# Row statistics moved by one row, and one scaling moved by one product, in a single-core graph attention kernel

## Chip, core and metric

One Trainium2 chip, of which one core is used. The metric is the device time of one execution in microseconds. A core has five engines that run beside each other, each through a list of instructions in a fixed order: TensorE (PE, with its weight loads PEld), VectorE (DVE), ScalarE (ACT), GpSimd (POOL) and SyncE (SP), which here issues nearly all DMA transfers. An instruction waits for semaphores of other engines; whatever stands behind it on its engine waits with it.

## What is computed

```
h = max(layernorm(x, over 768 features), 0)              # x: 128 graphs x 128 nodes x 768, float32
q, k, v = h @ Wq + bq, h @ Wk + bk, h @ Wv + bv          # 12 heads of 64, seen as 8 batches of 1024 rows
s = q k^T / sqrt(64) + beta * adj                        # within each graph: adj is 128 x 128 x 128
s = -9e15 where adj <= 0
out = x + softmax(s) v
```

In the kernel the unit is a graph of 128 nodes: attention runs between the nodes of one graph.

## The kernel before

**Groups, slices, products.** Four graphs make a group G; there are 32 groups, 0 to 31. For each group the three projections are computed in three slices: `qk0` (queries and keys of the first six heads), `v`, and `qk1` (queries and keys of the other six). The text calls them the first, second and third slice. From group 1 on a slice is 15 *products* (`product_z`, L521; the table at L66) of a fast matrix multiplication: each multiplies a prepared sum of blocks of the activations with a prepared sum of blocks of the weights, in 7 zones of two matmuls (28 instructions of TensorE, line L537). A product belongs to one of four *chains* a, b, c, d. A chain adds all its products up in one PSUM pair (two banks), and after each of its products the running sum is added to, or copied into, one or two of the six results (`home`) of the slice. So the next product of the same chain, usually three places later, can start only when that has been done: PSUM must have been read before TensorE adds to it again.

**Reading PSUM out.** The first product that goes into a result copies it with ScalarE (L555 for five zones and two times L557, with the bias, in the q and k slices; L551 on VectorE and L552 on ScalarE in the second slice). Later products are added by VectorE (L561). When all products of a result are there, GpSimd decodes it (L577 to L580 for q and k, L588 to L592 for v; one of them per group on VectorE).

**PSUM pairs.** There are four in all, in a queue: `take` gets the oldest free one, `give` puts one back. Chains hold one from their first to their last product; scores and weighted sums take one for a short time.

**Attention of a group.** Scores (L614) are 32 matmuls behind a product. VectorE caps them, adds the mask and frees the pair (L622); ScalarE takes the exponential (L624). The weighted sums (`attend_steps`, L671) are woven into the zones of the next product; then ScalarE copies the row sums and the values out of PSUM (L680, L682) and frees the pair; one product later VectorE takes the reciprocal (L642) and ScalarE scales the result with it in 8 instructions (L654); some products later VectorE adds `x` (L696) and SP sends the result to memory (L700). The last argument of `attention` (`behind`) is the number of products after which the addition comes; the sending comes two later. With 5 or less the scaling follows in the product of the reciprocal; with 6 it follows one product later (L688 and L689).

**Layer normalization of the groups to come.** From group 2 on it is spread over the slices of the two groups before. For each of the four graphs of group G+2 one row of `x` (128 x 768, 384 KB) is loaded into one buffer (`load_row`, L402, on SP), and ScalarE takes its statistics there (`row_stats`: L409 the sum, L410 the mean, L411 the squares). The next row can be loaded only when the statistics of the last one are through. When all four are there, `row_moments` makes them into scale and shift (L416 on VectorE, L421 and L422 on GpSimd) and turns them into the layout of the blocks by a write to memory and a broadcast read (L427 `turned`, L428 `block`, both on SP, a given number of products after the call). In the next group, ScalarE applies them to the blocks of `x` (`norm`, L438), which were loaded separately (`load_x`, L189). VectorE transposes the blocks (L449), GpSimd and VectorE make the sums that the products need (L459 to L461, L454).

**Weights.** Of the 45 prepared weight sums 11 stay on chip; the other 34 are streamed from memory for each group, 448 KB each, into a ring of five buffers (`load_T`, L335): a buffer is loaded again when its product is through.

**What sets the order.** From the second slice of group 0 on, the order on each engine is the order in which the program issues the instructions. A slice is a list `todo` of work by product number: `then(n, f)` issues f behind the matmuls of product n, ahead of the reading out of that product; `then((n, "post"), f)` issues it behind the reading out and behind what trails it (the scaling L654, the exponential L624). `later(f, k)` issues f k products on. `run` (L784) walks through a slice:

```
for at, steps in enumerate(products):
    next(steps)                    # matmuls, with woven-in weighted sums; then the load of weights
    behind_product(at, todo)       # todo[at], masks, L680/L682, then what is due from later()
    next(steps)                    # L555/L557 or L551/L552 or L561
    trail()                        # L654, L624
    for f in todo.get((at, "post"), ()):
        f()
```

The change touches only the numbers in the loop over the groups, L1039 to L1109.

Of the kernel before, what the change touches and what calls it, by code (L numbers as in the profile page):

```python
# [125 lines left out]
def direct(ctx, tc, x, adj, wq, bq, wk, bk, wv, bv, beta, out, bad):  # L126
# [14 lines left out]
    NG = B // GRP  # L141
# [181 lines left out]
    def order_of(G, sl):  # L323
        return LORDER if G == NG - 1 and sl == "qk1" else ORDER[sl]
# [459 lines left out]
    def run(products, todo):  # L784
        for at, steps in enumerate(products):
            next(steps)
            behind_product(at, todo)
            next(steps)
            trail()
            for f in todo.get((at, "post"), ()):  # L790
                f()

    def slice_z(G, sl, todo):
        run([product_z(G, sl, n) for n in order_of(G, sl)], todo)
# [163 lines left out]
    def then(at, f, *args):  # L958
        todo.setdefault(at, []).append(lambda: f(*args))
# [9 lines left out]
    def attention(G, u, at, behind=5):  # L969
        for n, j in at:  # L970
            then(n - 3, load_xo, G, 3 * u + j)
            then((n, "post"), attend, G, 3 * u + j, behind)
# [12 lines left out]
    def sums_at(G, slots):  # L985
        for at, name in slots:
            then(at, sum_acts, G, name)
# [51 lines left out]
    for G in range(1, NG):  # L1039
        more = G + 1 < NG  # L1040
        todo.clear()
        then(3, scores, G - 1, 1, 2)
        then(5, scores, G - 1, 1, 0)
        then((6, "post"), scores, G - 1, 1, 1)
        attention(G - 1, 1, ((7, 2), (10, 0), (12, 1)))
        if G == 1:
            sums_at(1, ((0, "S6"), (1, "S7"), (2, "S0"), (5, "S5"), (7, "S14"), (9, "S11")))
            then((0, "post"), load_x, 2, 0)
            for g, at in enumerate((3, 7, 11)):
                then((at, "post"), row_stats, 2, g)  # L1050
                then((at, "post"), load_row, 2, g + 1)
        else:
            sums_at(G, ((0, "S7"), (1, "S0"), (4, "S5"), (7, "S14"), (9, "S11")))
            if more:
                for g in range(2):
                    for h in range(2):
                        then((2 * g + h, "post"), norm, G + 1, g, 2 * h, 2 * h + 2)
                turn_act(G + 1, ((8, "A01"), (9, "A00"), (11, "A02")), None)
                then((12, "post"), load_x, G + 1, 1)
                if G + 2 < NG:  # L1060
                    then((12, "post"), load_row, G + 2, 0)
        slice_z(G, "qk0", todo)

        todo.clear()
        then(0, scores, G, 0, 2)
        then(2, scores, G, 0, 1)
        then(7, scores, G, 0, 0)
        if more:
            then((11, "post"), add_raw, G + 1)
            if G == 1:  # L1070
                then((0, "post"), row_stats, 2, 3)
                then(1, row_moments, 2, 3, 4)
                for n, at in enumerate((6, 7, 8, 9)):
                    then((at, "post"), norm, 2, n // 2, n % 2 * 2, n % 2 * 2 + 2)
                turn_act(2, ((10, "A01"), (11, "A00"), (12, "A02")), 1)
                then((12, "post"), load_x, 2, 1)
            else:
                for n, at in enumerate((3, 4, 7, 8)):
                    then((at, "post"), norm, G + 1, 2 + n // 2, n % 2 * 2, n % 2 * 2 + 2)
                turn_act(G + 1, ((10, "A11"),), 1)  # L1080
                for at, name in ((4, "A01"), (5, "A00"), (6, "A02")):
                    then(at, inner, G + 1, name)
            if G + 2 < NG:
                if G == 1:
                    then((1, "post"), load_row, 3, 0)
                for g, at in enumerate((5, 10, 14) if G == 1 else (1, 5, 10)):
                    then((at, "post"), row_stats, G + 2, g)
                    if at < 14:
                        then((at + 1, "post"), load_row, G + 2, g + 1)
        slice_z(G, "v", todo)  # L1090

        todo.clear()
        if not more:
            break
        attention(G, 0, ((3, 2), (9, 1), (12, 0)))
        if G == 1:
            for n, at in enumerate((0, 1, 2, 3)):
                then((at, "post"), norm, 2, 2 + n // 2, n % 2 * 2, n % 2 * 2 + 2)
            turn_act(2, ((4, "A10"), (5, "A11"), (6, "A12")), 1)
            then((0, "post"), load_row, 3, 3)  # L1100
        else:
            turn_act(G + 1, ((1, "A10"), (4, "A12")), 1)
        sums_at(G + 1, ((6 + (G == 1), "S1"), (7 + (G == 1), "S9"), (8 + (G == 1), "S2"), (11, "S6"), (13, "S10")))
        bias(G + 1, 0, 2, 4)
        if G + 2 < NG:
            then((4, "post"), row_stats, G + 2, 3)
            then(7, row_moments, G + 2, 3, 6)
            then((6, "post"), load_x, G + 2, 0)
        slice_z(G, "qk1", todo)  # L1109

    for at, f, *args in (
# [149 lines left out]
```

## Time and profile before

| | |
|---|---|
| runs | 2769.48 us median of 3 (2767.8 to 2770.46) |
| profiled execution | 2771.61 us, span of its trace 2769.8 us |
| busy: TensorE / weight loads | 2681.8 us (97%) / 2566.1 us (93%) |
| busy: VectorE / ScalarE / GpSimd | 2166.7 us (78%) / 1764.1 us (64%) / 2098.4 us (76%) |
| granted TensorE clock | 0.997 |
| DMA | 721.72 MB, 261 GB/s on average |

A group takes about 84 us: 84.60 us and 84.10 us for the two groups from 1556.60 us and from 1641.10 us, of which TensorE is busy for 82.39 and 82.41. In the timeline a row has the start, the duration, the engine, the line, the operation, output and input, the number of instructions in it, and in brackets the idle time of the engine before it with what ended it. Consecutive matmuls overlap (a row of one product lasts 1.70 us, yet the next starts 1.53 us after it), so lost time of TensorE is read from the distances between starts.

### The profile page before, as it was taken

The numbers are of one execution on the slowest core, as the hardware profiler recorded it, in microseconds if no ns is written. First come the engines' busy times: TensorE is split into PE (matmuls) and PEld (weight loads), VectorE is DVE, ScalarE is ACT, GpSimd is POOL, SyncE is SP. The second block draws the span as 40 slices with busy tenths as digits, with TensorE's granted clock in tenths as the row PEclk, the third lists the DMA queues.
The fourth block names the chain that finished last, engine by engine and source line by source line (L and its number), as shares of the span: only waits on it lengthen the run. The fifth ranks groups of instructions, "written<-read, shape, count | busy, mean of one in ns | idle before, by whom it ended". The sixth has DMA issues, their size and how long they took to land.

```text
span 2769.8 us, 121511 instructions
## 1 busy us (share of the span) xinstructions
PE 2681.8 (97%) x52029; PEld 2566.1 (93%) x52029; DVE 2166.7 (78%) x2693; ACT 1764.1 (64%) x4612; POOL 2098.4 (76%) x3046
## 2 busy tenths in 40 slices
PE   9989999999999999999999999999999999999997
PEld 7789999999999999999999999999999999999997
DVE  6868877777877778877788777778777888777885
ACT  1476666666666766666666666666667666666653
POOL 4767778777778777787777787777777777877774
PEclk9999999999999999999999999999999999999999
DMA  8788889888888888888888888888888888888875
GB/s 214 259 257 260 263 262 275 264 264 271 256 274 273 263 265 266 265 274 264 270 264 263 267 272 266 267 261 254 273 264 270 267 265 260 273 265 275 248 230 161
DMA packets 530341, 721.72 MB, mean 261 GB/s; under 512 B 105980, under 2 KB 374024, under 8 KB 529800
## 3 DMA queue, kind: packets, MB, share of 16 engines
q1 hardware_dynamic: 528640, 713.12, 83.9%
q8 instruction: 412, 6.75, 0.9%
q10 hardware_dynamic: 1160, 0.79, 0.2%
q14 instruction: 129, 1.06, 0.1%
HBM read 647.73 MB, written 66.05 MB: 258 GB/s over the span
## 4 chain that ended last, share of the span: by engine, by line
PE 59%; DVE 12%; ACT 12%; POOL 7%; issue 4%; DMA 3%; SPq 0%; ACTq 0%; DVEq 0%; POOLq 0%
PE pair L537 49%; PE pair L614 6%; DVE home L561 4%; PE pair L671 4%; ACT e L654 4%; DMA sbig<-in_x_dram 2%; ACT home L555 1%; ACT sbig L409 1%; DVE sbig L454 1%; ACT home L557 1%; ACT sbig L411 1%; DVE sbig L561 1%; POOL home L578 1%; DVE home L577 1%; POOL home L577 1%
## 5 line engine op out<-in xcount | busy, mean ns | idle before, releaser
L561 DVE TENSOR_TENSOR home<-home,pair 128x896 f32<-128x896 f32 x810 | 862.8, 1076 | 327.9 <-PE pair L537 222.1
L537 PE MATMUL pair<-sbig,T_qk 128*64 128x128 f32 x13888 | 886.9, 273 | 32.3 <-ACT home L557 23.7
L537 PEld LDWEIGHTS pair<-sbig,T_qk 128*64 128x64 f32 x13888 | 752.0, 137 | 52.3 <-ACT home L557 33.5
L654 ACT ACTIVATE e<-e,sm 128x64 f32<-128x64 f32 x1512 | 381.7, 336 | 188.0 <-DVE sm L642 187.3
L577 POOL TENSOR_TENSOR home<-home 128x256 f32<-128x256 f32 x299 | 240.4, 804 | 293.6 <-DVE home L561 285.9
L537 PE MATMUL pair<-A,T_qk 128*64 128x128 f32 x6076 | 414.6, 273 | 0.0
L537 PE MATMUL pair<-T_v,sbig 128*64 128x128 f32 x6944 | 413.9, 274 | 0.0
L671 PE MATMUL pair<-v,e 128*64 128x65 f32 x6048 | 399.5, 221 | 2.3 <-DVE e L622 2.3
L537 PEld LDWEIGHTS pair<-T_v,sbig 128*64 128x64 f32 x6944 | 385.4, 137 | 5.3 <-issue 4.0
L555 ACT ACTIVATE home<-pair 128x640 f32<-128x640 f32 x325 | 227.9, 701 | 215.1 <-PE pair L537 212.8
L671 PEld LDWEIGHTS pair<-v,e 128*64 128x64 f32 x6048 | 357.1, 137 | 5.6 <-DVE e L622 2.7
L537 PEld LDWEIGHTS pair<-A,T_qk 128*64 128x64 f32 x6076 | 330.1, 137 | 5.5 <-issue 5.5
L580 POOL TENSOR_TENSOR home<-home 128x256 f32<-128x256 f32 x299 | 283.1, 947 | 23.4
L622 DVE SCALAR_TENSOR_TENSOR e<-pair,biasT 128x1024 f32<-128x1024 f32 x189 | 230.4, 1219 | 43.5 <-PE pair L614 42.2
L578 POOL TENSOR_TENSOR home<-home 128x256 f32<-128x256 f32 x299 | 229.3, 767 | 23.4
L624 ACT ACTIVATE e<-e 128x1024 f32<-128x1024 f32 x189 | 200.4, 1061 | 62.4 <-DVE e L622 47.9
L680 ACT ACTIVATE sm<-pair,tiny 128x8 f32<-128x8 f32 x189 | 50.0, 264 | 294.5 <-PE pair L671 294.4
L537 PE MATMUL pair<-sbig,res_qk 128*64 128x128 f32 x3472 | 213.1, 274 | 22.4 <-ACT home L557 15.9
L438 ACT ACTIVATE x<-x,block 128x192 f32<-128x192 f32 x480 | 232.1, 543 | 3.9 <-DMA x<-in_x_dram 2.1
L537 PEld LDWEIGHTS pair<-sbig,res_qk 128*64 128x64 f32 x3472 | 189.1, 137 | 29.7 <-ACT home L557 21.6
L579 POOL TENSOR_TENSOR home<-home 128x128 f32<-128x128 f32 x299 | 194.1, 649 | 23.4
L557 ACT ACTIVATE home<-pair,bqk 128x128 f32<-128x128 f32 x650 | 202.2, 369 | 0.0
(188 smaller groups left out, 4687.0 us busy)
## 6 DMA issues: line engine op xcount, KB each, us to landing
T_qk<-kept_qk SPq DMA_DIRECT2D x713, 448.0 KB, 4.9
T_v<-kept_v SPq DMA_DIRECT2D x341, 448.0 KB, 5.9
xo<-in_x_dram SPq DMA_DIRECT2D x189, 256.0 KB, 4.5
out_dram<-xo SPq DMA_DIRECT2D x189, 256.0 KB, 4.9
x<-in_x_dram SPq DMA_DIRECT2D x248, 192.0 KB, 5.8
sbig<-in_x_dram SPq DMA_DIRECT2D x120, 384.0 KB, 5.1
kept_qk<-prep_qk SPq DMA_DIRECT2D x23, 448.0 KB, 3.3
adj<-in_adj_dram SPq DMA_DIRECT2D x128, 64.0 KB, 3.7
```

The source lines that it names most:

```text
L438: nc.scalar.activation(t, t, AF.Relu, bias=shift[G, n], scale=rstd[G, n])
L537: nc.tensor.matmul(p[q:q + HD, at, :], lhs[:, q:q + HD], rhs, start=(first and at % 4 == 0), stop=True, skip_group_check=True)
L555: nc.scalar.activation(t[:, 0:5], p[:, 0:5], AF.Copy, scale=float(sign))
L557: nc.scalar.activation(t[:, at], p[:, at], AF.Identity, bias=bqk[:, of, oc:oc + 1], scale=float(sign))
L561: nc.vector.tensor_tensor(t, t, p[:, 0:7], op)
L577: e.tensor_tensor(t[:, 1:4:2], t[:, 1:4:2], twice(5), ALU.add)
L578: e.tensor_tensor(t[:, 2:5:2], t[:, 2:5:2], twice(1), ALU.add)
L580: e.tensor_tensor(t[:, 0:7:6], t[:, 0:7:6], twice(2), ALU.add)
L622: nc.vector.scalar_tensor_tensor(e, ps, SCORE_CAP * ISCALE, bias, op0=ALU.min, op1=ALU.add)
L624: trailing.append(lambda: nc.scalar.activation(e, e, AF.Exp, scale=1.0 / ISCALE))
L654: nc.scalar.activation(o[:, r, b, 0:HD], pa[:, r, b, 0:HD], AF.Copy, scale=t[:, 1, r, b:b + 1])
L671: nc.tensor.matmul(pa[q:q + HD, 2 * g + i, :], k[:, q:q + HD], vt[G, "v", r, h // 4][:, 4 * g + h % 4, :], start=True, stop=True, skip_gro ...
```

## The change

Statistics and row loads of group G+2 start earlier by one row, and one attention's scaling comes a product later:

- For groups 3 to 31 (computed beside groups 1 to 29) the four statistics of a group change their places. From group 2 on they stood behind products 1, 5 and 10 of the second slice and 4 of the third; they now stand behind product 8 of the first slice and 1, 5 and 10 of the second. Their row loads go from 12 (first slice), 2, 6 and 11 (second) to 10 (third slice of the group before), 9 (first), 2 and 6 (second).
- `row_moments` goes from product 7 of the third slice to 5, and its transfers from 3 and 6 products behind it to 6 and 9 products from it (the counts are the arguments of the call; the products are 9 and 12 before, 10 and 13 now).
- In group 1 the statistics of group 2 go from 3, 7, 11 (first slice) and 0 (second) to 2, 6, 10 and 14 (first), those of group 3 from 5, 10, 14 (second) and 4 (third) to 5, 11 (second) and 5, 9 (third), with their row loads; its `row_moments` goes from product 7 of the third slice to 10.
- The last weighted sum of the third slice (woven in behind product 12) has `behind` 6 in place of 5: its scaling L654, which followed product 14, follows product 0 of the next group's first slice; the addition goes from product 2 to 3 and the sending from 4 to 5.

```diff
@@ first slice (qk0) @@
         if G == 1:
             ...
-            for g, at in enumerate((3, 7, 11)):
+            for g, at in enumerate((2, 6, 10, 14)):
                 then((at, "post"), row_stats, 2, g)
-                then((at, "post"), load_row, 2, g + 1)
+                if g < 3:
+                    then((at, "post"), load_row, 2, g + 1)
         else:
             ...
                 if G + 2 < NG:
-                    then((12, "post"), load_row, G + 2, 0)
+                    then((8, "post"), row_stats, G + 2, 0)
+                    then((9, "post"), load_row, G + 2, 1)
         slice_z(G, "qk0", todo)
@@ second slice (v) @@
             if G == 1:
-                then((0, "post"), row_stats, 2, 3)
                 then(1, row_moments, 2, 3, 4)
             ...
             if G + 2 < NG:
                 if G == 1:
                     then((1, "post"), load_row, 3, 0)
-                for g, at in enumerate((5, 10, 14) if G == 1 else (1, 5, 10)):
+                for g, at in ((0, 5), (1, 11)) if G == 1 else ((1, 1), (2, 5), (3, 10)):
                     then((at, "post"), row_stats, G + 2, g)
-                    if at < 14:
+                    if g < 3:
                         then((at + 1, "post"), load_row, G + 2, g + 1)
         slice_z(G, "v", todo)
@@ third slice (qk1) @@
-        attention(G, 0, ((3, 2), (9, 1), (12, 0)))
+        attention(G, 0, ((3, 2), (9, 1)))
+        attention(G, 0, ((12, 0),), 6)
         if G == 1:
             ...
-            then((0, "post"), load_row, 3, 3)
+            then((5, "post"), row_stats, 3, 2)
+            then((5, "post"), load_row, 3, 3)
+            then((9, "post"), row_stats, 3, 3)
         ...
         if G + 2 < NG:
-            then((4, "post"), row_stats, G + 2, 3)
-            then(7, row_moments, G + 2, 3, 6)
+            then(*((10, row_moments, G + 2, 3, 5) if G == 1 else (5, row_moments, G + 2, 6, 9)))
             then((6, "post"), load_x, G + 2, 0)
+        if G + 3 < NG:
+            then((10, "post"), load_row, G + 3, 0)
         slice_z(G, "qk1", todo)
```

## The prediction

> **What bounds the kernel now.** I read the page first, then TensorE's waits, then one group instruction by instruction. Products are numbered 0 to 14 in each slice; G is the group being computed; times on a clock are microseconds from the span's start.
>
> ```profile
> PE 2681.8 (97%) x52029; PEld 2566.1 (93%) x52029; DVE 2166.7 (78%) x2693; ACT 1764.1 (64%) x4612; POOL 2098.4 (76%) x3046
> ```
>
> TensorE (PE) is never long idle, so a change that adds no matmul and removes none can only move the remaining 88 us. The waits of its weight loads (total, times, longest), between 300 and 2580 us:
>
> ```profile
> PEld pair L537 <- ACT home L557: 49.0, 64, 1.2
> ...
> PEld pair L537 <- ACT sbig L557: 11.5, 15, 1.2
> ```
>
> One cause leads: a product waits until ScalarE (ACT) has copied an earlier product of the same chain out of PSUM (L555 and two L557). In the timeline of TensorE for one group there are two such places (start, duration, ..., idle before and its releaser):
>
> ```profile
> 1636.95 1.70 PE L537 MATMUL pair<-A,T_qk 128*64 128x128 f32 x28
> 1638.47 1.70 PE L537 MATMUL pair<-sbig,res_qk 128*64 128x128 f32 x28
> 1641.15 1.97 PE L537 MATMUL pair<-sbig,T_qk 128*64 128x128 f32 x32 [0.98 <-ACT home L557]
> ...
> 1650.71 6.28 PE L537 MATMUL pair<-sbig,T_qk 128*64 128x128 f32 x112
> 1657.65 1.75 PE L537 MATMUL pair<-sbig,res_qk 128*64 128x128 f32 x28 [0.65 <-ACT home L557]
> ...
> 1660.36 3.28 PE L537 MATMUL pair<-sbig,T_qk 128*64 128x128 f32 x56
> ```
>
> A product follows its predecessor by 1.53 us (1636.95 to 1638.47). Product 9 of the third slice starts 2.68 after product 8: **wait A**, 2.68 - 1.53 = 1.15 us. The four products from 1650.71 (product 14 and the next group's first slice, 0 to 2) are through at 1656.83; product 3 starts at 1657.65: **wait B**, 0.82 us. Both recur at the same place in every steady group. ScalarE beside them:
>
> ```profile
> 1635.84 0.87 ACT L409 ACTIVATE sbig<-sbig 128x768 f32<-128x768 f32 x1
> ...
> 1638.00 2.00 ACT L654 ACTIVATE e<-e,sm 128x64 f32<-128x64 f32 x8
> 1639.91 0.68 ACT L555 ACTIVATE home<-pair 128x640 f32<-128x640 f32 x1
> 1640.50 0.60 ACT L557 ACTIVATE home<-pair,bqk 128x128 f32<-128x128 f32 x2
> ...
> 1654.48 2.02 ACT L654 ACTIVATE e<-e,sm 128x64 f32<-128x64 f32 x8 [2.80 <-DVE sm L642]
> 1656.41 0.69 ACT L555 ACTIVATE home<-pair 128x640 f32<-128x640 f32 x1
> ...
> 1657.49 0.98 ACT L438 ACTIVATE x<-x,block 128x192 f32<-128x192 f32 x2
> 1658.37 0.70 ACT L555 ACTIVATE sbig<-pair 128x640 f32<-128x640 f32 x1
> ```
>
> Wait A: the fourth row statistics (1635.84 to 1638.00, so 2.16 us by spacing) and the scaling L654 (1638.00 to 1639.91) stand ahead of product 6's copy, which ends at 1641.10; TensorE goes on at 1641.15. Wait B: the scaling of the last weighted sum, itself held until 1654.48, stands ahead of product 0's copy, which ends at 1657.60.
>
> **The change, part by part.** No instruction is added or removed: each engine has as many rows in the order of the changed program. Only places change.
>
> *Fourth statistics leave the third slice* (groups 2 to 29, 28 times). L654 can then start where L409 did, at 1635.84, and end at 1637.77; product 6 is through when product 7 starts, at 1636.95, so its copy runs 1637.8 to 1639.0, a microsecond before product 9 wants to start at 1640.0. Wait A goes: 28 x 1.15 = **-32.2**. In group 1 two statistics now stand in the third slice, one of them right behind that L654, so its wait A stays.
>
> *Last scaling one product later* (groups 1 to 30, 30 times). Product 0's copy no longer waits for VectorE's reciprocal; it starts when product 0 is through and ends some 1.6 us before product 3. Wait B goes: 30 x 0.82 = **-24.6**. What is late next is product 1's copy. After A is gone product 0 starts at 1652.24 - 1.15 = 1651.09, its copy at 1652.84 (1.75 later, as below at 1671.36 and 1673.11), L654 at about 1654.0, the two L438 at 1655.95, product 1's copy at 1656.85 to 1658.05. Product 4 wants it at 1655.68 + 2.71 = 1658.39 (2.71 is 1657.65 to 1660.36). It fits with 0.3 us. The addition that uses the scaled sum and the sending of the output go one product later too; VectorE has the same work in both orders.
>
> *First statistics enter the first slice, behind product 8* (groups 2 to 29). This is where a new wait arises. ScalarE, then TensorE, at that place before:
>
> ```profile
> 1671.58 0.27 ACT L680 ACTIVATE sm<-pair,tiny 128x8 f32<-128x8 f32 x1 [1.74 <-PE pair L671]
> 1671.74 0.59 ACT L682 COPY e<-pair 128x520 f32<-128x520 f32 x1
> 1673.11 0.70 ACT L555 ACTIVATE home<-pair 128x640 f32<-128x640 f32 x1 [0.78 <-PE pair L537]
> ...
> 1674.35 2.02 ACT L654 ACTIVATE e<-e,sm 128x64 f32<-128x64 f32 x8
> ```
> ```profile
> 1671.36 1.70 PE L537 MATMUL pair<-sbig,T_qk 128*64 128x128 f32 x28
> ...
> 1674.63 0.40 PE L671 MATMUL pair<-v,e 128*64 128x65 f32 x8
> ```
>
> The changed order on ScalarE is L680, L682, the statistics, L555 and L557 of product 9, L654. Product 9 closes its chain and gives its PSUM pair back; the next to take that pair, in the queue of four, is the weighted sum woven into product 11 (both are pair 75 in every group that I read in the changed order). L682 is through at 1672.33 (0.78 of idleness before 1673.11), and a next instruction overlaps its last 0.1; the statistics take 2.16, from about 1672.22 to 1674.38; L555 with its two L557 ends 1.19 later (1639.91 to 1641.10), at 1675.57. The weighted sum wanted its pair at 1674.63, and TensorE executes in order: it stands still until 1675.6. **Wait C**, 0.97 us; 28 x 0.97 = **+27.2**. Behind C stands all of TensorE; VectorE, GpSimd and the ScalarE instructions after L654 are released by TensorE and shift with it. The bounds: nothing, if the pair were another, and 2.16, the whole statistics.
>
> *The other statistics* (second slice, behind 1, 5 and 10) keep their places and change only their number.
>
> *Row loads.* Each is one 384 KB transfer on SP's queue. The one behind product 9 of the first slice must wait for the end of L411 at 1674.4, while the weight load after it waits for product 10 anyway (1674.42): at most its own half microsecond. The first row comes a whole slice earlier, behind product 10 of the third slice, and lands long before its use. I take 0; late weights would cost up to what a late transfer shows below.
>
> *Row moments* (one VectorE, two GpSimd instructions, two small transfers) go from product 7 to 5, their transfers from products 9 and 12 to 10 and 13.
>
> ```profile
> L416 DVE TENSOR_SCALAR verow<-strow x30: 417/690/721, 164.1 to 2567.1; 128x4 f32<-128x4 f32 x30
> ```
> ```profile
> 1635.64 1.09 DVE L561 TENSOR_TENSOR home<-home,pair 128x896 f32<-128x896 f32 x1 [0.96 <-PE pair L537]
> ```
> ```profile
> SPq L427 <- POOL row L422: 106.8, 29, 5.1
> ```
>
> L416's 0.69 us fits in front of product 5's addition (L561), where VectorE idles 0.96. SP now stands 106.8 us in all, 3.7 per group, for GpSimd's result; earlier powers and a later transfer take that away, but the weights queued behind were not late, so it pays nothing.
>
> *Group 1.* The statistics behind product 14 of its second slice go:
>
> ```profile
> 190.81 3.23 PE L537 MATMUL pair<-sbig,T_qk 128*64 128x128 f32 x56
> 195.32 1.75 PE L537 MATMUL pair<-A,res_qk 128*64 128x128 f32 x28 [1.28 <-ACT home L557]
> ```
>
> Two products from 190.81 are through at 193.87, so 1.45 us was lost and can return; one statistics in its first slice, now behind product 10, may cost half a microsecond. I take **-1** (from +1 to -3).
>
> **Sum:** -32.2 - 24.6 + 27.2 - 1 = -30.6. The profiled execution took 2771.61 us (span 2769.8): 2741.0. It lies 2.1 above the median of the runs, 2769.48; taking the same sum from that gives 2738.9. I forecast **2739**.
>
> **The rivals.** *Wait B is replaced.* With B gone TensorE comes to the scores of the first slice 0.82 us nearer to what feeds them (VectorE's masking frees their pair; GpSimd's decoding makes their operands):
>
> ```profile
> 1661.30 1.21 DVE L622 SCALAR_TENSOR_TENSOR e<-pair,biasT 128x1024 f32<-128x1024 f32 x1
> ```
> ```profile
> 1664.63 0.74 POOL L580 TENSOR_TENSOR home<-home 128x256 f32<-128x256 f32 x1
> ```
> ```profile
> 1663.57 1.10 PE L614 MATMUL pair<-home 64*64 64x128 f32 x32
> ...
> 1666.29 1.10 PE L614 MATMUL pair<-home 64*64 64x128 f32 x32
> ```
>
> The mask ends at 1662.51, 1.06 before its scores; the decoding ends at 1665.37, 0.92 before. After B is gone 0.24 and 0.10 remain. If the reordered VectorE work makes GpSimd slower by more than 0.1, B comes back in part; at the worst whole: -30.6 + 24.6 = -6.0, or 2763. GpSimd's own rows show that it can:
>
> ```profile
> 1658.44 1.17 POOL L577 TENSOR_TENSOR home<-home 128x256 f32<-128x256 f32 x1
> ...
> 1662.47 0.73 POOL L577 TENSOR_TENSOR home<-home 128x256 f32<-128x256 f32 x1
> ```
>
> One instruction takes 0.73 or 1.17. The Trainium skill, "SBUF — State Buffer", section "SBUF: two separate sides", says that a VectorE instruction with two SBUF inputs and a GpSimd instruction that reads SBUF exclude each other for their whole length. The two lengths agree with that rule; by it the addition moved past one L561 only changes which GpSimd instruction waits, and the sum stays.
>
> *C does not come*, because the pair is another or is free: 2739 - 27 = 2712. For it speaks only that no trace has shown C yet.
>
> *The slower one: the norms wait for their statistics.* The transfer L428 feeds L438 behind product 0, now issued a product later, behind a 384 KB row load (SP and ScalarE in two groups, and last the landing of the streamed weights T_qk):
>
> ```profile
> 1649.95 0.54 SPq L428 DMA_DIRECT2D block<-turned  x1
> ```
> ```profile
> 173.81 0.57 SPq L428 DMA_DIRECT2D block<-turned  x1
> ```
> ```profile
> 178.19 1.86 ACT L438 ACTIVATE x<-x,block 128x192 f32<-128x192 f32 x4 [1.75 <-DMA block<-turned]
> ```
> ```profile
> DMA to landing us min/median/max: 3.0/4.9/8.6
> ```
>
> At 173.81 it took 4.4 us to land. Before, the norms came 7.5 us after its issue (1657.49) and did not wait. In the changed kernel it can be issued when product 13 is through, at 1650.71 - 1.15 = 1649.56 and some 0.5 for SP, and L438 wants it at 1655.95: 5.9 us, and 0.3 more before product 4 suffers. Landing later than 6.2 stops TensorE; from 7.3 on (30.6 / 28 = 1.1 more) the change is a loss. The streamed weights (last row) need 4.9 in the median and 8.6 at the worst; at 8.0 the loss is 28 x 1.8 = 50, less 30.6: 2789.
>
> *It does nothing*: not so in the order of the instructions, but A and B could return at their neighbours; 2769.
>
> **How the numbers follow.** Forecast 0.60; B replaced in part or whole (2745 to 2763) 0.18; no C (2712) 0.08; norms late (2789) 0.11; nothing 0.03. The forecast's own range, 2730 to 2748, takes in group 1, a C of 0.75 to 1.2 and B returning by 0.1. For 8 in 10 I leave out the norms and most of "no C": 2726 to 2764. A difference of 0.2%, 5.5 us, is about the least that a measurement of this kernel can tell from none. Faster: 0.60 + 0.08 + 0.17 = 0.85; same 0.04; slower 0.11.
>
> **What would show it.** Right: no idle time before product 9 of the third and product 3 of the first slice; a new wait of about 1 us at L671 in product 11 of the first slice, released by L557, 28 times; groups 1.0 us shorter. Wrong: waits at L614 on L580 or L622 (B replaced); L438 waiting for the block transfer (norms late); L671 in product 11 without a wait (no C); or longer gaps at the streamed weights, which I cost at nothing.

## The result, and the profile after

| | before | after |
|---|---|---|
| median | 2769.48 us (2766.07 to 2771.0, 5 runs) | 2751.8 us (2745.79 to 2754.33, 5 runs) |
| profiled execution / its span | 2771.61 / 2769.8 us | 2751.8 / 2749.9 us |

The ratio is 0.9936, with a 95% interval of 0.9922 to 0.9951: 17.7 us faster by the medians. The forecast was 2739. The sign and the range for 8 in 10 (2726 to 2764) held; the forecast's own narrower range (2730 to 2748) did not, and 13 us of the gain did not come.

The first row of the profile page of the changed kernel:

```profile
PE 2671.3 (97%) x52029; PEld 2565.2 (93%) x52029; DVE 2194.7 (80%) x2693; ACT 1763.8 (64%) x4612; POOL 2107.5 (77%) x3046
```

The instruction counts are those of before. Yet VectorE (DVE) is busy 28 us longer (2166.7 before) and GpSimd (POOL) 9 us longer. The same instructions have become slower, and no step of the prediction had that.

The waits of the weight loads between 300 and 2580 us, of the changed kernel (us in total, times, longest), and then a row of the same view of the kernel before:

```profile
PEld pair L614 <- POOL home L580: 27.2, 52, 1.0
...
PEld pair L671 <- ACT home L557: 23.1, 22, 1.1
PEld pair L614 <- issue: 18.7, 109, 0.2
PEld pair L671 <- ACT sbig L557: 5.2, 5, 1.0
PEld pair L537 <- ACT home L557: 5.0, 24, 0.3
```
```profile
PEld pair L614 <- issue: 34.2, 165, 1.1
```

L537 hardly waits for ScalarE's copy any more (49.0 before, 5.0 now): waits A and B are gone. At L671 stand 22 + 5 waits of about a microsecond: wait C, as forecast. Two things are new. The scores (L614) wait 27.2 us, here put down to GpSimd. And their small waits without a releaser have shrunk from 34.2 to 18.7. TensorE's own waits, over the whole run, name another releaser for the first:

```profile
PE pair L614 <- DVE e L622: 21.6, 30, 1.4
PE pair L671 <- ACT home L557: 18.6, 23, 0.8
```

The timeline of TensorE for one group (start, duration, ..., idle before and its releaser):

```profile
1629.08 1.70 PE L537 MATMUL pair<-sbig,res_qk 128*64 128x128 f32 x28
1630.61 1.92 PE L537 MATMUL pair<-sbig,T_qk 128*64 128x128 f32 x32
...
1640.11 6.29 PE L537 MATMUL pair<-sbig,T_qk 128*64 128x128 f32 x112
1646.23 1.70 PE L537 MATMUL pair<-sbig,res_qk 128*64 128x128 f32 x28
...
1648.89 3.28 PE L537 MATMUL pair<-sbig,T_qk 128*64 128x128 f32 x56
1652.91 1.10 PE L614 MATMUL pair<-home 64*64 64x128 f32 x32 [0.74 <-DVE e L622]
...
1663.75 0.39 PE L537 MATMUL pair<-sbig,T_qk 128*64 128x128 f32 x4
1664.95 0.45 PE L671 MATMUL pair<-v,e 128*64 128x65 f32 x8 [0.81 <-ACT home L557]
```

Product 9 of the third slice follows product 8 by 1.53 us (1629.08 to 1630.61): A is gone. Four products take 4 x 1.53 = 6.12 us up to product 3 of the first slice (1640.11 to 1646.23): B is gone. The weighted sum in product 11 starts 1.20 after the product's first four matmuls, where 0.22 is usual in this timeline: C. And the scores behind product 5 start 4.02 us after 1648.89, where the kernel before took 3.21 (1660.36 to 1663.57): a new wait, **wait D**.

ScalarE at C:

```profile
1661.08 0.59 ACT L682 COPY e<-pair 128x520 f32<-128x520 f32 x1
1661.55 0.85 ACT L409 ACTIVATE sbig<-sbig 128x768 f32<-128x768 f32 x1
...
1663.70 0.68 ACT L555 ACTIVATE home<-pair 128x640 f32<-128x640 f32 x1
1664.28 0.61 ACT L557 ACTIVATE home<-pair,bqk 128x128 f32<-128x128 f32 x2
```

The statistics take 1661.55 to 1663.70 (2.15), the copy behind them ends at 1664.89, and TensorE goes on at 1664.95. VectorE and then GpSimd ahead of D, in the changed kernel:

```profile
1635.70 1.51 DVE L454 TENSOR_TENSOR sbig<-sbig,A 128x896 f32<-128x896 f32 x1
...
1639.20 1.59 DVE L454 TENSOR_TENSOR sbig<-A,A 128x896 f32<-128x896 f32 x1
...
1651.55 1.21 DVE L622 SCALAR_TENSOR_TENSOR e<-pair,biasT 128x1024 f32<-128x1024 f32 x1
```
```profile
1638.30 0.73 POOL L577 TENSOR_TENSOR home<-home 128x256 f32<-128x256 f32 x1
1639.11 0.73 POOL L578 TENSOR_TENSOR home<-home 128x256 f32<-128x256 f32 x1
1639.92 1.19 POOL L579 TENSOR_TENSOR home<-home 128x128 f32<-128x128 f32 x1
```

and the same two places in the kernel before:

```profile
1646.30 1.08 DVE L454 TENSOR_TENSOR sbig<-sbig,A 128x896 f32<-128x896 f32 x1
...
1649.48 1.08 DVE L454 TENSOR_TENSOR sbig<-A,A 128x896 f32<-128x896 f32 x1
```
```profile
1647.40 0.73 POOL L577 TENSOR_TENSOR home<-home 128x256 f32<-128x256 f32 x1
...
1649.56 1.59 POOL L580 TENSOR_TENSOR home<-home 128x256 f32<-128x256 f32 x1
```

Product 0 of the first slice starts at 1652.24 before and at 1640.11 + 1.53 = 1641.64 after. Against that, GpSimd's decoding (L577) starts 4.84 us ahead before, and only 3.34 us ahead after. VectorE's block sum S10 (L454, the later of the two rows) stands at nearly the same place (2.76 and 2.44 ahead), but takes 1.08 before, when it is GpSimd's L580 that is slow (1.59), and 1.59 after. The sum ahead of it has gone from 1.08 to 1.51. The mask L622 ends at 1652.76, just ahead of the scores that need its pair.

To see all the places at once I matched TensorE's 52,029 matmuls, which both kernels issue in the same order, by number, and took the change of the distances between their starts, averaged over groups 2 to 29. Every column is one profiled execution of a run, in us per group against the kernel before (the runs are told below):

| place | forecast | after | e1 | e2 | e3 | e4 | e6 | e10 | e12 | e14 |
|---|---|---|---|---|---|---|---|---|---|---|
| products 1, 2 of the first slice | 0 | -0.11 | -0.05 | -0.09 | -0.11 | -0.08 | **+2.58** | -0.01 | **+1.06** | -0.06 |
| product 3 (B) | -0.82 | -0.84 | **+0.94** | -0.84 | -0.84 | -0.84 | -0.78 | -0.84 | -0.82 | -0.84 |
| scores behind product 5 (D) | 0 | **+0.76** | 0.00 | +0.03 | +0.75 | 0.00 | 0.00 | +0.70 | +0.05 | **+0.46** |
| scores behind product 6 | 0 | 0.00 | 0.00 | +0.06 | 0.00 | **+0.85** | 0.00 | 0.00 | +0.07 | 0.00 |
| weighted sum in product 11 (C) | +0.97 | +1.03 | +1.03 | 0.00 | **0.00** | +1.03 | +1.03 | 0.00 | +1.04 | 0.00 |
| scores behind product 2 of the second slice | 0 | -0.46 | -0.36 | -0.02 | -0.45 | -0.39 | -0.40 | **+0.01** | -0.37 | -0.02 |
| product 9 of the third slice (A) | -1.15 | -1.20 | -1.20 | 0.00 | -1.20 | -1.20 | -1.20 | -1.20 | -1.20 | -0.01 |
| whole group | -1.00 | -0.80 | +0.24 | -0.77 | -1.62 | -0.54 | +1.35 | -1.38 | -0.19 | -0.54 |

Small changes at other places make up the rest of each sum.

### The profile page after: what moved, and what is told of

It is laid out like the page before. It is cut to its first block, busy times and chain, and to the rows that moved or that the text cites. A ratio compares the mean times of both kernels' runs of the same rounds, so it can differ in the third digit from the quotient of the medians.

```text
span 2749.9 us, 121542 instructions
## 1 busy us (share of the span) xinstructions
PE 2671.3 (97%) x52029; PEld 2565.2 (93%) x52029; DVE 2194.7 (80%) x2693; ACT 1763.8 (64%) x4612; POOL 2107.5 (77%) x3046
## 3 DMA queue, kind: packets, MB, share of 16 engines
q14 instruction: 130, 1.06, 0.1%
## 4 chain that ended last, share of the span: by engine, by line
PE 61%; DVE 16%; DMA 6%; ACT 6%; POOL 5%; issue 3%; SPq 0%; DVEq 0%; POOLq 0%; ACTq 0%
PE pair L537 51%; PE pair L614 5%; DVE home L561 5%; PE pair L671 5%; DVE sbig L454 5%; DMA turned<-row 2%; DMA T_qk<-kept_qk 2%; DVE e L622 2%; DVE xo L696 2%; ACT sbig L411 1%; ACT sbig L409 1%; DMA sbig<-in_x_dram 1%; DVE sbig L561 1%; ACT home L555 1%; ACT home L557 1%
## 5 line engine op out<-in xcount | busy, mean ns | idle before, releaser
L561 DVE TENSOR_TENSOR home<-home,pair 128x896 f32<-128x896 f32 x810 | 861.0, 1076 | 284.7 <-PE pair L537 187.2
L537 PE MATMUL pair<-sbig,T_qk 128*64 128x128 f32 x13888 | 886.1, 274 | 3.3 <-ACT home L557 2.2
L537 PEld LDWEIGHTS pair<-sbig,T_qk 128*64 128x64 f32 x13888 | 754.7, 137 | 16.8 <-ACT home L557 7.6
L654 ACT ACTIVATE e<-e,sm 128x64 f32<-128x64 f32 x1512 | 382.2, 342 | 108.2 <-DVE sm L642 108.0
L671 PE MATMUL pair<-v,e 128*64 128x65 f32 x6048 | 401.5, 222 | 27.4 <-ACT home L557 18.6
L577 POOL TENSOR_TENSOR home<-home 128x256 f32<-128x256 f32 x299 | 228.8, 765 | 259.1 <-DVE home L561 249.5
L537 PE MATMUL pair<-A,T_qk 128*64 128x128 f32 x6076 | 414.6, 273 | 0.0
L537 PE MATMUL pair<-T_v,sbig 128*64 128x128 f32 x6944 | 412.3, 273 | 0.0
L671 PEld LDWEIGHTS pair<-v,e 128*64 128x64 f32 x6048 | 356.0, 137 | 38.6 <-ACT home L557 24.1
L537 PEld LDWEIGHTS pair<-T_v,sbig 128*64 128x64 f32 x6944 | 383.7, 137 | 5.5 <-issue 5.2
L537 PEld LDWEIGHTS pair<-A,T_qk 128*64 128x64 f32 x6076 | 330.1, 137 | 5.5 <-issue 5.5
L580 POOL TENSOR_TENSOR home<-home 128x256 f32<-128x256 f32 x299 | 280.3, 938 | 23.5
L622 DVE SCALAR_TENSOR_TENSOR e<-pair,biasT 128x1024 f32<-128x1024 f32 x189 | 230.5, 1220 | 35.4 <-PE pair L614 35.4
L579 POOL TENSOR_TENSOR home<-home 128x128 f32<-128x128 f32 x299 | 216.4, 724 | 23.4
L438 ACT ACTIVATE x<-x,block 128x192 f32<-128x192 f32 x480 | 231.2, 538 | 4.4 <-DMA block<-turned 3.0
L537 PE MATMUL pair<-sbig,res_qk 128*64 128x128 f32 x3472 | 211.6, 273 | 0.5 <-DVE home L561 0.5
L614 PE MATMUL pair<-home 64*64 64x128 f32 x5312 | 187.8, 275 | 18.1 <-DVE e L622 18.1
```

The costliest lines, as they stand in the source:

```text
L438: nc.scalar.activation(t, t, AF.Relu, bias=shift[G, n], scale=rstd[G, n])
L537: nc.tensor.matmul(p[q:q + HD, at, :], lhs[:, q:q + HD], rhs, start=(first and at % 4 == 0), stop=True, skip_group_check=True)
L561: nc.vector.tensor_tensor(t, t, p[:, 0:7], op)
L577: e.tensor_tensor(t[:, 1:4:2], t[:, 1:4:2], twice(5), ALU.add)
L580: e.tensor_tensor(t[:, 0:7:6], t[:, 0:7:6], twice(2), ALU.add)
L614: nc.tensor.matmul(ps[k:k + HD, i, g * N:(g + 1) * N], keys[r, k:k + HD], queries[r], start=True, stop=True)
```

## The experiments

The question is where D comes from. **Theory 1**: VectorE has no slack left, because the stretch from A to D is 1.15 us shorter and its work isn't. **Theory 2**: VectorE and GpSimd meet; GpSimd does not become earlier by as much as TensorE, its decoding falls beside VectorE's sums, and each holds the other up. The rest of the runs tell apart the parts of the change that I had costed at nothing.

**e1: the statistics and loads alone** (the changed kernel with the scaling back).

```diff
-        attention(G, 0, ((3, 2), (9, 1)))
-        attention(G, 0, ((12, 0),), 6)
+        attention(G, 0, ((3, 2), (9, 1), (12, 0)))
```

> The changed kernel with the last scaling put back to where it was (behind 5), the shifted statistics kept. The sum as forecast (each wait has its own fixed price): wait B returns with 0.82 us per group and the new wait at the scores of the first slice (D, 0.81 us) goes, since B stands ahead of it; about 2752 us. Theory 'VectorE has no slack left': since wait A went, VectorE is later against TensorE, its reciprocal for the last weighted sum too, and wait B comes back longer, about 1.7 us per group: about 2777 us, slower than before.

2782.99 us, ratio 1.0042 (1.0025 to 1.006): slower. TensorE's waits:

```profile
PE pair L537 <- ACT home L557: 38.8, 27, 1.8
```

and ScalarE at B:

```profile
1662.43 2.02 ACT L654 ACTIVATE e<-e,sm 128x64 f32<-128x64 f32 x8 [3.80 <-DVE sm L642]
```

A is gone and C has come, as in the whole change; B has grown by 0.94 to 1.76 us. The scaling ahead of product 0's copy waits for VectorE's reciprocal, and VectorE has not become earlier with TensorE: the scaling starts 3.24 us after product 0's start (1659.19), and 2.24 after it in the kernel before (1654.48 and 1652.24). Most of what A gave is lost at B, and C comes on top.

**e2: the scaling alone** (the kernel before with these two lines).

```diff
-        attention(G, 0, ((3, 2), (9, 1), (12, 0)))
+        attention(G, 0, ((3, 2), (9, 1)))
+        attention(G, 0, ((12, 0),), 6)
```

> The kernel before with the last scaling alone one product later (behind 6), statistics as before. Theory 'VectorE has no slack left': wait A stays and keeps VectorE its idle time, so B goes (0.82 x 30) and no wait D comes: about 2745 us. If D is simply what follows when B goes (the scores are reached earlier): 2767 us.

2748.48 us, ratio 0.9924 (0.9898 to 0.9949). Only B changes, by -0.84, and there is no D. This part alone is worth as much as the whole change. The two parts alone give +11.6 and -22.9 us against the kernel before on their chip (2771.38), together -11.3, and the whole change -17.7. They aren't independent, since the one decides whether the other's VectorE work is waited for.

**e3: the third group's statistics behind product 7** in place of 8.

```diff
-                    then((8, "post"), row_stats, G + 2, 0)
-                    then((9, "post"), load_row, G + 2, 1)
+                    then((7, "post"), row_stats, G + 2, 0)
+                    then((8, "post"), load_row, G + 2, 1)
```

> The changed kernel with the first statistics behind product 7 in place of 8 of the first slice (row load behind 8). If wait C is only the statistics standing between L682 and the copy of product 9, it goes: 28 x 1.03 = 29 us, about 2723 us; the idle time of ScalarE ahead of L680 (1.74 us) takes most of the statistics, so L682 comes 0.4 later and product 10 still finds its pair. Rival: wait C also gave TensorE time for what it lost at the scores of the second slice before (0.4 us per group, put down to issue); then this returns: about 2734 us. Rival: the later L682 stops product 10 by about as much as C: 2745 us or more.

2727.44 us, ratio 0.985 (0.9823 to 0.9876). C is gone to 0.00, and little else has moved: behind product 7 the statistics end before product 9's copy is due. The row load moved with them, but e10 below puts it elsewhere and C stays away, so it is the statistics' place that counts. C's mechanism was right, and it was avoidable. D stays at 0.75.

**e4: the sum S5 one product later**, behind the mask instead of ahead of it.

```diff
-            sums_at(G, ((0, "S7"), (1, "S0"), (4, "S5"), (7, "S14"), (9, "S11")))
+            sums_at(G, ((0, "S7"), (1, "S0"), (5, "S5"), (7, "S14"), (9, "S11")))
```

> The changed kernel with one sum of VectorE (S5, line 454) moved from product 4 to product 5 of the first slice, behind the masking of the first scores. Theory 'VectorE is late with the mask (L622), which holds the PSUM pair of the next scores': wait D goes, 28 x 0.8 = 22 us, about 2730 us. Theory 'GpSimd is late with the decoding (L580)', as the row of the weight loads says: D stays, about 2752 us.

2757.44 us, ratio 0.9949 (0.9932 to 0.9967). TensorE's waits:

```profile
PE pair L614 <- POOL home L580: 18.1, 26, 0.8
```

With VectorE's mask out of the way D is gone, and 0.85 us of wait stands one product on, now for GpSimd's decoding. Both engines are late there by about the same. This fits neither a full VectorE alone nor a full GpSimd alone.

**e6: the row moments back** to product 7, as before.

```diff
-            then(*((10, row_moments, G + 2, 3, 5) if G == 1 else (5, row_moments, G + 2, 6, 9)))
+            then(*((10, row_moments, G + 2, 3, 5) if G == 1 else (7, row_moments, G + 2, 3, 6)))
```

> The changed kernel with the row moments alone put back to product 7 of the third slice (transfers 3 and 6 products on, as before). Theory 'phase': the two GpSimd instructions of the moments, now early, push a decoding (L577 to L580) onto VectorE's sums (L454), which took 1.5 in place of 1.08 us and used up VectorE's idle time; put back, the sums are short again, L622 comes 0.4 to 0.9 us earlier and wait D shrinks to between 0 and 0.4 us: 2729 to 2740 us. Theory 'less time': VectorE is late only because TensorE comes 1.2 us sooner; D stays, 2752 us.

2812.51 us, ratio 1.0165 (1.0138 to 1.0191): the median is 60.7 us above the changed kernel's. SP's queue (start and duration), and TensorE a little later in the same group:

```profile
980.91 0.42 SPq L601 DMA_DIRECT2D xo<-in_x_dram  x1
986.87 0.56 SPq L427 DMA_DIRECT2D turned<-row  x1
987.53 0.42 SPq L335 DMA_DIRECT2D T_qk<-kept_qk  x1
...
988.52 0.45 SPq L402 DMA_DIRECT2D sbig<-in_x_dram  x1
989.07 0.44 SPq L335 DMA_DIRECT2D T_qk<-kept_qk  x1
```
```profile
991.65 1.75 PE L537 MATMUL pair<-sbig,T_qk 128*64 128x128 f32 x28 [0.29 <-DMA T_qk<-kept_qk]
995.33 0.88 PE L537 MATMUL pair<-sbig,T_qk 128*64 128x128 f32 x12 [1.94 <-DMA T_qk<-kept_qk]
```

SP stands 5.5 us (981.33 to 986.87) at L427 until GpSimd has the powers. The weight loads and the row load queue behind it and go out in a heap, and products 1 and 2 wait for their weights (+2.58 per group). D shows as 0.00 only because TensorE is late by more than that already; so this run says nothing on the wait itself.

**e7 and e9: the row moments back in e3 and in e8** (the line of e6 again).

> The kernel with the first statistics behind product 7 (no wait C), and the row moments put back to product 7 of the third slice. Phase: 2705 to 2716 us. Less time: 2727 us, as without the second edit.

> Both edits on the kernel with the first statistics behind product 7: moments back and sums earlier. If D is VectorE's lateness, it is gone: 28 x 0.8 under 2727, about 2705 us. If GpSimd's own work is the bound: 2727 us.

2803.3 us, ratio 1.0134 (1.0115 to 1.0153), and 2797.87 us, ratio 1.0118 (1.0094 to 1.0141). The same wait for weights, in kernels without C.

**e12: e6 with the new row load behind product 14** of the third slice in place of 10.

```diff
-            then((10, "post"), load_row, G + 3, 0)
+            then((14, "post"), load_row, G + 3, 0)
```

> e6 (row moments back behind product 7 of the third slice, 2812 us, the streamed operand T of the first slice's products 1 and 2 late) with the third slice's new row load behind product 14 instead of 10. Theory 'SP stands at L427': SP waits in order for GpSimd's powers and the operand's loads stand behind that, so the row load's place changes nothing: about 2812 us. Rival 'the row load is ahead of the operand's loads and takes the transfer time': the load comes after them now, and most of the 2.3 us per group goes: 2750 us or less.

2773.58 us, ratio 1.0012 (1.0 to 1.0024). TensorE's waits, to be read against e6's 61.8 us:

```profile
PE pair L537 <- DMA T_qk<-kept_qk: 23.5, 28, 2.5
```

Neither side was right alone. Products 1 and 2 lose 1.06 per group in place of 2.58: about 1.5 us came from the 384 KB row load standing ahead of a weight load, and what is left against the changed kernel (1.06 and -0.11, so 1.2) I put down to SP's standing at L427. The sizes are rough: the profiled execution took 2764.78 us, 8.8 less than this run's median, so 1.06 is rather low. So the earlier place of the moments, which I had costed at nothing, is what makes the earlier row load bearable.

**e8: three of VectorE's sums (S1, S9, S2) one product earlier** in the third slice, on e3, to test theory 1.

```diff
-... (6 + (G == 1), "S1"), (7 + (G == 1), "S9"), (8 + (G == 1), "S2"), ...
+... (5 + 2 * (G == 1), "S1"), (6 + 2 * (G == 1), "S9"), (7 + 2 * (G == 1), "S2"), ...
```

> The kernel with the first statistics behind product 7, and VectorE's sums S1, S9, S2 one product earlier in the third slice (5, 6, 7 in place of 6, 7, 8; group 1 as it was), so that VectorE uses the 0.64 us that it idles ahead of the reading out of product 5. Phase or less time: VectorE is up to 0.64 us earlier from there on, if nothing else holds it up before the scores; D shrinks from 0.8 to about 0.2: 2711 us. If GpSimd's own work is the bound, D stays: 2727 us.

2725.18 us, ratio 0.9844 (0.9827 to 0.9861), the fastest of all and not to be told from e3. D stays at 0.73. VectorE came earlier by 0.7 us, stood idle for 0.7 us some 7 us ahead of the first slice, waiting for TensorE's next product, and was then slow again in the sum S6, in S10 and in its own decoding. So VectorE still has slack 7 us ahead of the first slice and becomes late only behind that, which speaks against theory 1.

**e11: one decoding of the second slice on VectorE** instead of GpSimd, on e3.

```diff
-... nc.vector if (sl, n) == ("qk1", 13) else nc.gpsimd ...
+... nc.vector if (sl, n) in (("qk1", 13), ("v", 6)) else nc.gpsimd ...
```

> e3 with one of the second slice's six decodings (behind the product with A00) given to VectorE, which stands free there, instead of GpSimd. It takes some 2.9 us of each group off GpSimd's queue ahead of the third slice. Theory 'GpSimd's backlog': the wait at the scores in the first slice's product 5 (0.75 us per group, new with the change) comes from GpSimd running its decoding beside VectorE's block sum, so that both are late by the same amount; with the backlog shorter that overlap goes and the wait with it: 2727 - 28 x 0.75 = 2706 us. Rival 'VectorE alone': its queue between the third slice's end and the mask is too full whatever GpSimd does, so the wait stays: about 2727 us. Third: VectorE has no room in the second slice either and a copy of a product is late there: above 2735 us, with a new wait in the second slice.

2738.51 us, ratio 0.9882 (0.9861 to 0.9903): slower than e3. It did not do what it was made for. The decoding taken away stood too early; GpSimd's five others still follow each other without a pause, and it came to the decoding ahead of D not earlier but 0.44 us later against TensorE (2.83 us ahead of product 0 in place of 3.27). D fell from 0.75 to 0.66, and VectorE, loaded in the second slice, gave a new wait of 0.56 per group there. It settles nothing.

**e14: GpSimd made later by itself**, on e2, which has no D. Two of GpSimd's operations are done twice, behind the row powers. VectorE's work and its order are those of e2. (The added lines shift the lines below: L454 is L458 here, L577 to L580 are L581 to L584, L622 is L626.)

```diff
             nc.gpsimd.tensor_tensor(t[:, 1], mean, t[:, 0], ALU.mult)
+            if first == 3 and G > 3:
+                w = wide[G - 1, "A12"]
+                nc.gpsimd.tensor_tensor(w[:, 0:2], w[:, 7:8].to_broadcast([P, 2, P]), w[:, 5:7], ALU.subtract)
+                nc.gpsimd.tensor_tensor(w[:, 2], w[:, 6], w[:, 0], ALU.subtract)
```

> e2 (the scaling alone, 2748 us, without the wait at the scores of the first slice's product 5) with two of GpSimd's operations done twice: the first two of the block A12's inner differences (0.73 and 0.46 us as the trace of e2 has them), again behind the row powers L421 and L422, so that SP's L427 isn't later by them. GpSimd then begins the decoding of the result (0,2) about 1.3 us later against TensorE, at some 3.5 us ahead of the first slice instead of 4.84, where it stands in the kernel with the change. VectorE's own work is that of e2. Theory 'VectorE and GpSimd meet': the decoding falls beside VectorE's sum S10 and VectorE's own decoding, which get longer, the mask L622 is late, and the wait at the scores of product 5 comes as in the whole change, 0.76 us per group: 2748 + 28 x 0.76 = 2769 us, with the sum S10 at 1.5 to 1.6 us instead of 1.08. Rival 'VectorE's own queue, because the third slice is shorter': GpSimd's place doesn't matter, about 2748 us and S10 at 1.08 us.

2754.91 us, ratio 0.9967 (0.9953 to 0.9981), and D is there, 0.46 us per group where 0.76 was expected; the whole group is 0.23 longer than in e2, since small changes elsewhere take the rest. The two added operations themselves run beside a VectorE addition with a PSUM input and do not lengthen it. VectorE and GpSimd of e2:

```profile
968.48 1.08 DVE L454 TENSOR_TENSOR sbig<-A,A 128x896 f32<-128x896 f32 x1
...
980.19 1.21 DVE L622 SCALAR_TENSOR_TENSOR e<-pair,biasT 128x1024 f32<-128x1024 f32 x1
```
```profile
968.02 0.46 POOL L579 TENSOR_TENSOR home<-home 128x128 f32<-128x128 f32 x1
968.56 1.59 POOL L580 TENSOR_TENSOR home<-home 128x256 f32<-128x256 f32 x1
```

and of e14, with TensorE's wait:

```profile
969.67 1.64 DVE L458 TENSOR_TENSOR sbig<-A,A 128x896 f32<-128x896 f32 x1
...
982.07 1.21 DVE L626 SCALAR_TENSOR_TENSOR e<-pair,biasT 128x1024 f32<-128x1024 f32 x1
```
```profile
969.63 0.73 POOL L582 TENSOR_TENSOR home<-home 128x256 f32<-128x256 f32 x1
970.44 1.19 POOL L583 TENSOR_TENSOR home<-home 128x128 f32<-128x128 f32 x1
```
```profile
PE pair L618 <- DVE e L626: 11.9, 28, 0.5
```

In e2 VectorE's S10 begins at 968.48, 0.08 before GpSimd's L580; S10 takes 1.08 and L580, which needs 0.73 elsewhere, takes 1.59. In e14 GpSimd's L582 begins at 969.63, 0.04 before S10; L582 takes its 0.73 and S10 takes 1.64. Then S10 is ahead of L583, which takes 1.19 in place of 0.46. The one that begins first is not slowed, and the other waits for most of it (it ends 0.13 to 0.14 us sooner than if it began its short length at the first one's end). VectorE's own decoding follows into GpSimd's L583 and L584, and the mask starts 9.63 us after product 0's start in e14 and 8.94 after it in e2 (product 0 starts at 972.44 and 971.25): 0.69 us late, of which 0.46 reaches TensorE. Theory 2 is shown as a cause of D: GpSimd 1.2 us later (its decoding starts 4.84 us ahead of product 0 in e2, 3.62 in e14), with VectorE's work as it was, makes it. In the changed kernel the mask starts 9.91 after product 0's start, 0.97 later than in e2, and D is 0.76; both pairs leave a slack of 0.21 to 0.23.

The Trainium skill, "SBUF — State Buffer", section "SBUF: two separate sides", calls the port pair that VectorE and GpSimd share "an **exclusive lock**, not a bandwidth split": whichever starts first has it for its whole instruction. The rows of e2 and e14 agree, down to the order of the starts 0.04 and 0.08 us apart.

**e10: e3 with the second row's load back behind product 12** of the first slice, where the kernel before loaded a row. What was open is the gain at the scores behind product 2 of the second slice.

```diff
-                    then((8, "post"), load_row, G + 2, 1)
+                    then((12, "post"), load_row, G + 2, 1)
```

> e3 (third group's statistics at 7) with the steady load of the second row block back behind product 12 of the first slice, where the kernel before issued its load, instead of behind 8. What is open is the 0.3 to 0.4 us per group of small waits ahead of the second slice's scores (L614, put down to issue) that the change as a whole has lost and that the scaling alone (e2) has not. Theory 'the place of the row load': with the load back at 12 they return, 28 x 0.33 = 9 us, so about 2736 us. Rival 'the statistics' place or the moments': the load is free to move, about 2727 us, and those waits stay as short as in e3.

2729.95 us, ratio 0.9857 (0.9841 to 0.9874). By the medians the run is only 2.5 us over e3 and not to be told from it, but the trace decides: the gain of 0.45 per group is gone (+0.01), and the waits of a microsecond are back:

```profile
PE pair L614 <- issue: 5.2, 11, 1.0
```

So the gain came with the earlier row load, and not with the statistics or the moments. The view names no releaser ("issue"), but the packets in the trace do. Instructions come in loads of 16 KB on a DMA queue of their own (q8, of the kind "instruction"). In the kernel before and in e10 the wait stands in 20 and in 24 of the groups 2 to 29, at a matmul that moves on by one every two groups (the 14th of 32 in group 2, the 27th in group 29), and in each of them TensorE goes on 1.23 to 1.59 us after such a load has landed. With the row load behind product 12 this instruction load begins, in the median, 0.07 us before (kernel before) and 0.14 us after (e10) the start of product 2; in the changed kernel and in e3 it begins 1.44 and 1.58 us before it, and the wait stands in no group and in one. So, by these times, TensorE waits here for its own instructions, and they are late when the row load is on its way at that time. The row load's place was tried; the step through the instruction load is read from the packets.

## Why the prediction was right and wrong

- **Wait A** went: 1.20 per group, 28 x 1.20 = -33.6 us (forecast -32.2). The ScalarE arithmetic held.
- **Wait B**, at product 3 itself, went: 0.84 per group, 28 x 0.84 = -23.5 us over groups 2 to 29 (forecast -24.6 over 30). e2 shows it alone. Product 1's copy fitted in, as worked out.
- **Wait C** came, at the forecast place, by the forecast releaser: 1.03 per group, +28.8 us (forecast +27.2). e3 and e10 show its mechanism: the statistics behind product 7 instead of 8 remove it.
- **Wait D** is the step that failed. It stood among the rivals ("wait B is replaced"), with the right places, the right slacks (0.24 at the mask; the runs give 0.21 to 0.23) and a price of up to 24.6, but I gave it 0.18 and left it out of the sum: "the addition moved past one L561 only changes which GpSimd instruction waits, and the sum stays". That looked at the order on VectorE alone. With A gone TensorE and VectorE come to this place earlier, while GpSimd is still working off the second slice's decodings one behind the other; "GpSimd and the ScalarE instructions after L654 are released by TensorE and shift with it", which I wrote of wait C and took for granted at A, does not hold for an engine with a backlog. So GpSimd began the decoding 3.34 instead of 4.84 us ahead, and now it was VectorE that waited. The rule of the Trainium skill that I cited there held; I had its consequence the wrong way round. The rival's condition was off too: I gave it for B's going, but with B gone alone (e2) the place costs 0.03; in the change it is A's going that brings GpSimd too late. The cost: 28 x 0.76 = +21.3 us. Of the 0.97 us by which the mask is late, e14 shows 0.69. The other 0.28 I put down to the sum ahead of S10 (1.08 to 1.51): the row powers now run ahead of an earlier decoding of GpSimd and push it beside that sum. The runs with the moments back (e6, e7, e9, e12) bear that out only in part: the sum takes 1.08 again, but GpSimd's decoding then starts 3.06 us ahead of product 0, S10 takes 1.39, and VectorE's decoding ends 1.29 us after product 0's start, against 1.42 in the changed kernel and 0.43 in e2 (medians of 26 groups). So the earlier moments account for some 0.13, and the rest comes without them.
- **The row loads**, costed at nothing, paid: the scores behind product 2 of the second slice 28 x 0.46 = -12.9 us (e10), through no step of mine. That 2751.8 lies well inside the range for 8 in 10 is partly luck: 2739 and wait D alone make 2760, and this gain took more than half of D back.
- **The row moments**, "it pays nothing": in the kernel before no weights were late behind L427, but inside the change the step fails. With the new row load ahead of the weights, the old place costs 2.15 us per group (1.35 against -0.80; e6).
- **Group 1**: -2.5 us in this profile (93.86 to 91.33 us), forecast -1, from +1 to -3.
- **The norms** did not wait. The waits ahead of L438 in the changed kernel hold, of the transfer:

```profile
  DMA block<-turned: 3.0, 2
```

  Two waits in the whole run. That rival is out, and so are "C does not come" and "it does nothing".

The sum over groups 2 to 29, by the table: 28 x (-0.11 - 0.84 + 0.76 + 1.03 - 0.46 - 1.20) = -23.0, and 28 x -0.80 = -22.4 with the small rest. With group 1 (-2.5) and a start-up that was 4.3 us longer in this profile, -20.6; the profiled executions differ by 19.8. Of the 10.8 us between that and the forecast sum of -30.6, D less the two gains that I had not seen makes 21.3 - 12.9 - 3.1 = 5.3, and the start-up 4.3. The 3.1 (products 1 and 2) is no gain of each group: in the profile before, late weights cost up to 1.8 us there in three of the 28 groups.

## What to carry to other kernels

When a stall is removed, ask of each other engine whether it was released by the stalled engine or working off a queue of its own: only the first kind becomes earlier too, and every overlap between the two kinds changes. A neighbour on a shared resource whose slack is 0.1 to 0.24 us is part of the sum and not a rival, when the change shifts the two engines against each other by more than that. And try the parts of a change alone: here the scaling alone gave as much as all of it, and the first statistics and their row load one product earlier (e3) more than doubled the gain, to a ratio of 0.985.

## What the runs showed of the hardware

- A VectorE addition of two SBUF blocks (L454, 128x896) takes 1.08 us alone and up to 1.6 where it meets GpSimd. All of one form, shortest, median, longest in ns, in the kernel before and then in the changed one:

```profile
L454 DVE TENSOR_TENSOR sbig<-A,A x93: 1075/1084/1599, 124.9 to 2683.0; 128x896 f32<-128x896 f32 x93
```
```profile
L454 DVE TENSOR_TENSOR sbig<-A,A x93: 1079/1477/1603, 127.5 to 2661.2; 128x896 f32<-128x896 f32 x93
```

  The median alone has moved from 1084 to 1477, which one can read from the profile before any timeline: the same instructions, which now more often begin second. In the timeline of the group shown above the additions with one PSUM input (L561) stay at 1.04 to 1.09 us beside the same GpSimd work.
- A queue in order, on SP, makes a wait for a 0.2 us GpSimd instruction as costly as the transfers behind it: 5.5 us of standing, 2.58 us per group at TensorE with a 384 KB load ahead of the weights (e6), and 1.06 without it (e12).
- TensorE can stand for its own instructions: up to 1.4 us per group at the scores behind product 2 of the second slice, when a 16 KB instruction load lands late (kernel before, e2, e10, e14; read from the packets).
- The phase up to group 1's first product, in which the programs do not differ, ended at 127.2 us in the profile of the kernel before, at 131.5 in that of the changed one, and between 126.2 and 133.0 in all fourteen. A difference of 4 us between two single profiles is no effect.
